# Four kinds of side work beside a transformer: Mamba gets buffers of its own, and the list scheduler reserves accumulator banks for the eldest piece

## The chip, the core and the metric

The kernel runs on one core of a Trainium2 chip. The core has a matrix engine (TensorE, PE in the profile), a vector engine (VectorE, DVE), a scalar engine that evaluates functions (ScalarE, ACT), a programmable engine (GpSimd, POOL) and a queue engine that here issues nearly all DMAs (SyncE, SP). Each engine runs its own instructions in the order in which the program gives them, and waits on semaphores. Matmuls write to PSUM, of which the program has eight banks of 128 x 512 words: seven rotate, one holds small words.

The metric is the device time of one execution in microseconds; lower is better. A measurement is the median of several executions.

## The reference: what is computed

The input `u` is 4 sequences of 1024 positions with 128 channels. Four layers, each as `x = x + layernorm(layer(layernorm(x)))`:

```
# 1 Mamba (selective scan), 16 states
dt = softplus(u W_x[:64] W_dt + b_dt);  B, C = u W_x[64:80], u W_x[80:96]
h[t] = exp(dt[t] * -exp(A_log)) * h[t-1] + dt[t] * u[t] * B[t]
y = sum over states of h * C  +  u * D
# 2 experts: the 2 best of 8 by a router, softmax over the two logits
y = sum over 2 of weight * (gelu(x W_up + b_up) W_down + b_down)     # 128 -> 512 -> 128
# 3 dynamic convolution, 16 heads, 31 taps, causal
w = softmax over taps of (x w_lin);  y[t] = sum over k of w[t, k] * x[t - 30 + k]
# 4 transformer of 6 layers; half of the channels are shifted by one position before each part
for i in range(6):
    x = attention(shift(x)) + x      # 16 heads of 64, windows of 32 and the one before,
                                     # q and k normalised, scaled, rotated
    x = W2 (a * gelu(gate)) + x      # layernorm, 128 -> 2 x 341 -> 128
```

All arrays are float32.

## The kernel before

**Units of work.** A *block* is half a sequence, 512 positions; there are eight, numbered 0 to 7, two a sequence. Mamba, convolution and (in part) the experts work on blocks. A *tile* is 128 positions of one sequence in one transformer layer; there are 4 x 6 x 8 = 192, in order of sequence, layer, position. The transformer can begin with a sequence when both its blocks have gone through Mamba, experts and convolution.

**Three phases.** `sandwich` (L410) makes the generators of the work and merges them. First Mamba on block 0, with the steps of `prepare` (L1141) between its own; then Mamba on block 1, all eight experts on block 0 (`all_experts`, L777) and the rest of `prepare`; then convolution on block 0 and all experts on block 1. Everything else goes along with the transformer, in `Transformer.run` (L1471). `prepare` makes, for each of the six layers, the product of value and output weights (`wvod`) and the scaled rotation tables (`rotd`), and stores them in DRAM, from where each layer loads them later.

**What goes along.** `run` loops over the tiles. For each it turns queries and keys, works out scores, mixes values, and projects the tile after next; after each half sequence of four tiles comes the feed-forward part. Four times a tile it calls `along(i, part)`, which advances the lines of side work. A `Line` (L1564) has a list of jobs with a first and last tile; a job is given out step by step, so that its share of cost follows the share of time. Before the change there are two lines, one of experts and one of everything else (M is Mamba, E experts for two blocks with only the chosen ones, `chosen_experts`, L856; C is convolution):

```
experts = [(E, (2, 3), 18, 30), (E, (4, 5), 56, 78), (E, (6, 7), 84, 118)]
others = [(C, 1, 0, 2.6), (M, 2, 2.6, 11), (M, 3, 11, 18), (M, 4, 18, 30)]
others += [(C, 2, 30, 38), (C, 3, 38, 46), (M, 5, 46, 56), (M, 6, 56, 67)]
others += [(M, 7, 67, 78), (C, 4, 78, 87), (C, 5, 87, 97), (C, 6, 118, 130)]
others += [(C, 7, 130, 144)]
```

**The order on the engines.** None of these calls reaches an engine at once. `Order` (L144) records each as a `Unit` with its engine, an estimated cost, and edges to the units whose data or buffers it needs; matmuls that belong together form one unit. `arrange` (L275) then builds the final order: in each step it looks at the units whose predecessors are all given out, takes on each engine the earliest possible start (and the smallest index among those within `NEAR` of it), and gives out the earliest of all. Three rules bear on the change. A unit may not lie more than `AHEAD` = 500 indices past the oldest one not yet given out. A unit that needs a PSUM bank gets it only if two more stay free, except the oldest such unit. And a bank is fixed only here, when its first unit is given out. On the chip the order on each engine stays as arranged, whatever is late.

**Buffers.** `Rings` (L387) hands out SBUF buffers by tag, `bufs` of them in turn. The tag `near` has three buffers of 128 x 2048 words (`big`, L612). A Mamba block takes all three for its operands, states and products; a convolution tile takes two, one for each half of the 31 taps, and loads its 31 shifted copies of the rows into them by DMA. Both also use the tags `cxn` and `cxT`. Expert weights (514 KB an expert) have three buffers (`ewt`), two loaded ahead.

**Mamba** (`mamba`, L615) is a chain of 16 states: the product of a spread row of B with `dtu` on VectorE, a scan on VectorE (`tensor_tensor_scan`), the product with a spread row of C, and a sum on GpSimd. **Convolution** (`conv`, L1023) does, for each of four tiles, a softmax over taps, four products on GpSimd, two sums on GpSimd, and a sum over taps on VectorE; after the four it normalises and adds the block, stores it, and writes the transformer's input `hs`. **`chosen_experts`** scatters the block's rows into a list by expert (16 indirect DMAs), goes through 23 tiles of the list, fetching each tile's weights by an indirect DMA, and gathers the results. **`layernorm`** (L554) takes statistics on VectorE; it applies them on ScalarE if the source lies in SBUF, and on VectorE, four instructions, if it lies in PSUM.

Almost every instruction carries the line of the recorder that gives it out (L357), so the profile's groups are told apart by their tiles' names.

Of the kernel before, what the change touches and what calls it, by code (L numbers as in the profile page):

```python
# [88 lines left out]
class Bank:  # L89
    def __init__(self, like):  # L90
        self.like, self.ap, self.left, self.writes, self.reads = like, None, 0, [], []


class Unit:
# [4 lines left out]
        "end", "index", "table", "both", "given",  # L99
    )  # L100

    def __init__(self, engine, index):
# [4 lines left out]
        self.table, self.both, self.given = None, False, False  # L107
# [36 lines left out]
class Order:  # L144
# [6 lines left out]
    NEAR = {"tensor": 0.05, "vector": 0.05, "scalar": 0.25, "gpsimd": 0.40, "sync": 1.0}  # L151
    TABLE = {"Exp": "exp", "Gelu": "gelu", "Ln": "ln"}
# [7 lines left out]
    def bank(self):  # L160
        return Late(Bank(self.psum[0]))
# [6 lines left out]
    def take(self, engine, op, args, kw):  # L168
# [7 lines left out]
        if u is None or u.engine != engine:  # L176
            u = Unit(engine, len(self.units))
            self.units.append(u)
            if self.open is not None:
                raise ValueError("another engine in a unit")  # L180
# [20 lines left out]
    forced = None  # L201
# [73 lines left out]
    def arrange(self):  # L275
# [6 lines left out]
        oldest, needy, k_needy = 0, [u for u in units if u.banks], 0  # L282
        free = list(self.free)
        result = []
        while len(result) < len(units):
            while units[oldest].given:
                oldest += 1
            while k_needy < len(needy) and needy[k_needy].given:
                k_needy += 1
            eldest = needy[k_needy] if k_needy < len(needy) else None  # L290
            best = None
            for e, line in ready.items():
                found = []
                for u in line:
# [3 lines left out]
                    if u.banks:  # L298
                        n = len(u.banks)
                        if len(free) < n or (u is not eldest and len(free) < n + 2):  # L300
# [15 lines left out]
            if best is None:  # L316
                raise ValueError("no unit can be given out")
# [12 lines left out]
            for b in u.banks:  # L330
                b.ap = self.psum[free.pop(0)[1]]
# [3 lines left out]
            for b in u.uses:  # L335
                b.left -= 1
                if not b.left:
                    free.append((u.end + 0.08, b.slot))
# [34 lines left out]
class Together:  # L373
# [3 lines left out]
    def __enter__(self):  # L377
        o = self.order
        o.open = Unit("tensor", len(o.units))
        o.units.append(o.open)  # L380
# [29 lines left out]
def sandwich(ctx: ExitStack, tc: tile.TileContext, io: dict, out: bass.AP):  # L410
# [4 lines left out]
    prepare = t.prepare()  # L415
    for _ in c.mamba(0):
        next(prepare, None)
    merge([(c.mamba(1), MAMBA), (c.all_experts(0), ALL), (prepare, 2.0 * DEPTH)])
    merge([(c.conv(0), CONV), (c.all_experts(1), ALL)])
# [24 lines left out]
class Common:  # L444
# [91 lines left out]
    def bank(self, name):  # L536
        return self.nc.bank()
# [16 lines left out]
    def layernorm(self, dst, src, n):  # L554
# [14 lines left out]
        if src.space == PSUM:  # L569
            nc.vector.tensor_copy(mean, mv[:, :, 0])  # L570
            for g in range(n):
                nc.vector.tensor_scalar(
                    dst[:, g, :],
                    src[:, g, :],
                    mean[:, g : g + 1],
                    rs[:, g : g + 1],
                    ALU.subtract,
                    ALU.mult,
                )
        else:  # L580
# [31 lines left out]
    def big(self):  # L612
        return self.sb.tile([P, 4 * BLK], F32, "near", bufs=3)

    def mamba(self, k):  # L615
# [5 lines left out]
        big = [self.big() for _ in range(3)]  # L621
        uT, dt, y, dtu = [big[0][:, i * BLK : (i + 1) * BLK] for i in range(4)]
        ex, w, spare = [big[1][:, i * BLK : (i + 1) * BLK] for i in range(3)]
        parts = big[1][:, 3 * BLK :].bitcast(BF16)[:, :BLK]
        abs_, hs = [[big[2][:, (2 * i + e) * BLK : (2 * i + e + 1) * BLK] for e in range(2)] for i in range(2)]
        hcs = [spare, self.sb.tile([P, BLK], F32, "cxT")]
        dtr = y[:RANK]
        xn = self.norm(x, "m", "cxn")
# [40 lines left out]
        for n in range(STATE):  # L669
            ab = abs_[n % 2]  # L670
            nc.scalar.activation(ab, dt, AF.Exp, scale=self.a_neg[:, n : n + 1])
            h = hs[n % 2]
# [5 lines left out]
                h, ab, db, state if j else 0.0, ALU.mult, ALU.add  # L678
# [1013 lines left out]
```

## Time and profile before

| what | value |
|---|---|
| median of 4 runs | 4307.79 us (4303.37 to 4312.76) |
| the profiled execution | 4303.24 us, of which 4301.1 us from its first to its last instruction (the span) |
| mean granted TensorE clock | 0.945 |
| busy in the span: PE, weight loads, DVE | 3824.6, 2734.8, 3664.0 us |
| busy in the span: ACT, POOL | 2491.6, 2964.2 us |
| DMA | 260.45 MB, mean 61 GB/s |
| scores of tile 0 begin | 355.8 us |

The profile's page gives, by engine, the busy time and its course over 40 equal slices of the span. Other views of the same execution give groups of equal instructions (how many, how long in total and each, and for what the engine stood idle before them), waits by pairs of engines, and busy time by stretches of the span. PE's times are those of matmuls, weight loads have a row of their own and overlap them. A record of an instruction can overlap the next one's, so a group's busy time is less than its count times its mean.

### The profile page before, as it was taken

Reading aid. Unit: us, or ns where it says so; the run is one execution under the profiler, and the core shown is the slowest. Engines: PE = TensorE matmul, PEld = TensorE weight load, DVE = VectorE, ACT = ScalarE, POOL = GpSimd, SP = SyncE. Lnnn points to the kernel's source line nnn. Section 1 sums busy time; section 2 is a strip of 40 time slices with the busy share of each in tenths; the row PEclk is TensorE's granted clock in tenths of the full one; section 3 lists DMA queues with packets and bytes.
Section 4 is the critical chain, followed back from the end, with each engine's and each line's share of the span. In section 5 each row is a group of like instructions: output and inputs, shape, how many; then the busy total and the mean of one; then the engine's idle time right before and its main releaser. Section 6 shows DMA issues by size and latency. Waiting matters only on the chain. (4 is left out here: it accounts for less than half of the span.)

```text
span 4301.1 us, 111840 instructions
## 1 busy us (share of the span) xinstructions
PE 3824.6 (89%) x45298; PEld 2734.8 (64%) x45317; DVE 3664.0 (85%) x9478; ACT 2491.6 (58%) x4572; POOL 2964.2 (69%) x1826
## 2 busy tenths in 40 slices
PE   4856788889889889899998889999999999999997
PEld 2644455667656556577666567776667677777775
DVE  5636899986899899988998978788999998989986
ACT  4533555556555656577655556675556566666654
POOL 4468666675798765767687885666978866666653
PEclk6877899999999999999998999999999999999998
DMA  5522000023212100122122221221121111001010
GB/s 187 179 106 84 21 22 20 22 74 111 80 61 95 44 25 26 44 81 81 42 85 70 77 73 55 67 63 61 64 72 51 54 32 34 30 24 34 26 33 11
DMA packets 131596, 260.45 MB, mean 61 GB/s; under 512 B 15440, under 2 KB 91528, under 8 KB 123144
## 3 DMA queue, kind: packets, MB, share of 16 engines
q1 hardware_dynamic: 118072, 210.68, 14.9%
q0 software_dynamic: 13008, 42.62, 3.3%
q8 instruction: 357, 5.85, 0.6%
q14 instruction: 159, 1.30, 0.1%
HBM read 223.63 MB, written 29.62 MB: 59 GB/s over the span
## 5 line engine op out<-in xcount | busy, mean ns | idle before, releaser
L357 POOL TENSOR_TENSOR r<-r,rb 128x1024 f32<-128x1024 f32 x384 | 909.6, 2376 | 373.5 <-DVE rb L357 307.9
L357 POOL TENSOR_TENSOR r<-r,root 128x1024 f32<-128x1024 f32 x384 | 722.7, 1903 | 195.7 <-DVE root L357 179.3
L357 PE MATMUL bank<-wqk,hs 128*128 128x512 f32 x1536 | 776.0, 630 | 62.6 <-DVE at L357 32.0
L357 PEld LDWEIGHTS bank<-zT,wvo 128*128 128x128 f32 x6144 | 722.7, 194 | 90.4 <-issue 50.5
L357 PE MATMUL bank<-zT,wvo 128*128 128x128 f32 x6144 | 730.1, 277 | 10.5 <-ACT zT L357 8.3
L357 ACT ACTIVATE sq<-bank 128x512 f32<-128x512 f32 x768 | 442.0, 599 | 378.1 <-PE bank L357 191.1
L357 ACT COPY zT<-bank 128x512 f32<-128x512 f32 x768 | 404.7, 594 | 400.1 <-PE bank L357 394.9
L357 DVE TENSOR_TENSOR r<-bank,rot 128x512 f32<-128x512 f32 x768 | 522.9, 681 | 86.5 <-PE bank L357 39.6
L357 POOL TENSOR_TENSOR at<-at,sm 128x1024 f32<-128x1024 f32 x192 | 365.6, 1904 | 310.4 <-DVE sm L357 150.1
L357 DVE TENSOR_TENSOR rb<-bank,rot 128x512 f32<-128x512 f32 x768 | 520.9, 680 | 47.8 <-ACT sq L357 34.5
L357 DVE TENSOR_REDUCE words<-sq 128x8 f32<-128x512 f32 x768 | 526.2, 685 | 12.4 <-ACT sq L357 4.9
L357 PEld LDWEIGHTS bank<-wqk,hs 128*128 128x128 f32 x1536 | 273.5, 197 | 349.9 <-issue 166.7
L357 PE MATMUL bank<-aT,xw 64*128 64x256 f32 x3072 | 443.5, 410 | 21.9 <-DVE near L357 6.2
L357 PE MATMUL bank<-ident,r 128*128 128x128 f32 x3072 | 401.0, 279 | 47.4 <-POOL r L357 23.6
L357 PEld LDWEIGHTS bank<-ident,r 128*128 128x128 f32 x3072 | 353.3, 144 | 131.1 <-issue 63.4
L357 PEld LDWEIGHTS bank<-aT,xw 64*128 64x128 f32 x3072 | 299.2, 194 | 173.6 <-issue 52.5
L357 PEld LDWEIGHTS bank<-kT,qT 64*32 64x32 f32 x24576 | 262.1, 106 | 126.8 <-issue 113.6
L357 ACT COPY qT<-bank 128x512 f32<-128x512 f32 x384 | 226.0, 596 | 176.6 <-PE bank L357 175.2
L357 PE MATMUL bank<-kT,qT 64*32 64x64 f32 x24576 | 300.9, 227 | 21.3 <-issue 21.0
L357 DVE TENSOR_REDUCE mx<-bank 128x8 f32<-128x512 f32 x384 | 255.2, 681 | 68.8 <-PE bank L357 68.5
L357 PE MATMUL bank<-fxn,w 128*128 128x512 f32 (+1 forms) x576 | 275.3, 607 | 9.3 <-ACT fxn L357 5.5
L357 ACT ACTIVATE at<-at 128x1024 f32<-128x1024 f32 x192 | 203.2, 1058 | 119.0 <-DVE at L357 83.9
(180 smaller groups left out, 6781.1 us busy)
## 6 DMA issues: line engine op xcount, KB each, us to landing
near<-rows SPq DMA_DIRECT2D x32, 1024.0 KB
near<-rows SPq DMA_DIRECT2D x32, 960.0 KB
rot<-rotd SPq DMA_DIRECT2D x192, 128.0 KB
wqk<-in_Wqkv SPq DMA_DIRECT2D x48, 512.0 KB
wvo<-wvod SPq DMA_DIRECT2D x24, 1024.0 KB
ewt<-in_w_ex SPq DMA_DIRECT2D x16, 514.0 KB
w<-in_W SPq DMA_DIRECT2D x24, 341.0 KB
rb<-in_rot SPq DMA_DIRECT2D x12, 512.0 KB
```

The lines of the kernel that those rows point to most:

```text
L357: getattr(engine, op)(*map(real, args), **{k: real(v) for k, v in kw.items()})
```

## The change

Six things change together.

1. A Mamba block's operands come from nine buffers of its own (`m0` to `m8`); block 1 borrows the transformer's `r0`, `r1` and `at`, which are not in use yet. It uses `cxn` and `cxT` no more, the scan writes over its own multiplier, and `near` has two buffers. Tags `ewt`, `ey`, `sq` and `xw` lose one of three as well; experts load one ahead in place of two.
2. Four lines go along with the transformer: experts, convolution, Mamba, layer preparation. Mamba on block 2 moves to the phase before, next to convolution on block 0 and the experts on block 1.
3. `prepare` does layer 0 alone; layers 1 to 5 are the fourth line, in halves through the experts' buffers.
4. `layernorm` applies its result on ScalarE for every source.
5. In the first sequence convolution finishes each tile by itself (normalise, add, store, turn), in the others the block as before; the steps are now in `finish`.
6. `arrange`: units that are recorded while lines advance are marked `side`. The oldest unit, from which `AHEAD` counts, is the oldest that is not `side`. The eldest unit that needs banks is kept for each of the two kinds: the elder of the two takes a bank with none to spare, the other with one, all others with two; no more than three banks are held by projections (`qk`); if nothing can be given out, the reserve is waived for that step.

```diff
 class Order:
+    MOST = {"qk": 3}
...
-            while units[oldest].given:
+            while oldest + 1 < len(units) and (units[oldest].given or units[oldest].side):
                 oldest += 1
-            while k_needy < len(needy) and needy[k_needy].given:
-                k_needy += 1
-            eldest = needy[k_needy] if k_needy < len(needy) else None
+            for line in needy:
+                while line and line[-1].given:
+                    line.pop()
+            eldest = [line[-1] for line in needy if line]
+            first = min(eldest, key=lambda u: u.index, default=None)
...
-                        if len(free) < n or (u is not eldest and len(free) < n + 2):
+                        if len(free) < n + (0 if u is first or stuck else 1 if u in eldest else 2):
+                            continue
+                        name = u.banks[0].name
+                        if held.get(name, 0) >= self.MOST.get(name, 9):
                             continue
...
-    prepare = t.prepare()
-    for _ in c.mamba(0):
-        next(prepare, None)
-    merge([(c.mamba(1), MAMBA), (c.all_experts(0), ALL), (prepare, 2.0 * DEPTH)])
-    merge([(c.conv(0), CONV), (c.all_experts(1), ALL)])
+    merge([(c.mamba(0), MAMBA), (t.prepare(), 4.0)])
+    merge([(c.mamba(1), MAMBA), (c.all_experts(0), ALL)])
+    merge([(c.conv(0), CONV), (c.all_experts(1), ALL), (c.mamba(2), MAMBA)])
...
         if src.space == PSUM:
-            nc.vector.tensor_copy(mean, mv[:, :, 0])
-            for g in range(n):
-                nc.vector.tensor_scalar(
...
-        else:
+            pass
+        if True:
             nc.vector.scalar_tensor_tensor(mean, mv[:, :, 0], -1.0, rs, ALU.mult, ALU.mult)
...
     def big(self):
-        return self.sb.tile([P, 4 * BLK], F32, "near", bufs=3)
+        return self.sb.tile([P, 4 * BLK], F32, "near", bufs=2)
...
-        big = [self.big() for _ in range(3)]
...
+        if k == 1:
+            pairs = [self.sb.tile([P, 2, BLK], F32, f"r{i % 2}", bufs=2) for i in range(4)]
+            pieces = [pair[:, e, :] for pair in pairs for e in range(2)]
+            parts = self.sb.tile([P, 2, BLK], F32, "at", bufs=2)[:, 0, :]
+        else:
+            pieces = [self.sb.tile([P, BLK], F32, f"m{i}") for i in range(8)]
+            parts = self.sb.tile([P, BLK // 2], F32, "m8")
...
             nc.vector.tensor_tensor_scan(
-                h, ab, db, state if j else 0.0, ALU.mult, ALU.add
+                h, h, db, state if j else 0.0, ALU.mult, ALU.add
             )
...
-            w = self.sb.tile([P, 2 * UP + NUC], F32, "ewt", bufs=3)
+            w = self.sb.tile([P, 2 * UP + NUC], F32, "ewt", bufs=2)
...
-        ahead = [fetch(0), fetch(1)]
+        ahead = [fetch(0)]
...
-            if i + 2 < nt:
-                ahead.append(fetch(i + 2))
+            if i + 1 < nt:
+                ahead.append(fetch(i + 1))
...
+        size = 1 if b == 0 else 4
...
+            if g % size == size - 1:
+                self.finish(k, x, y, slice(g + 1 - size, g + 1))
...
+    def prepare_layer(self, l):
+        for j in range(2):
+            both = self.sb.tile([P, 8, D], F32, "exn")
+            wv, wo = both[:, :4], both[:, 4:]
+            dma(out=wv, in_=io["WvT"][l][:, 4 * j : 4 * j + 4])
...
+            for e in range(2):
+                wvo = self.sb.tile([P, BLK], F32, "eT")
+                nc.scalar.copy(wvo, pair[e])
+                dma(
+                    out=self.wvod[l][:, e, 4 * j : 4 * j + 4, :].rearrange("p a d -> p (a d)"),
+                    in_=wvo,
+                )
...
-        experts = [(E, (2, 3), 18, 30), (E, (4, 5), 56, 78), (E, (6, 7), 84, 118)]
+        experts = [(E, (2, 3), 8, 26), (E, (4, 5), 52, 70), (E, (6, 7), 98, 118)]
+        mambas = [(M, 3, 0, 8), (M, 4, 10, 32), (M, 5, 32, 52), (M, 6, 52, 74), (M, 7, 74, 98)]
+        convs = [(C, 1, 0, 2.6), (C, 2, 26, 35), (C, 3, 35, 44), (C, 4, 70, 80), (C, 5, 80, 90), (C, 6, 118, 127), (C, 7, 127, 138)]
+        layers = [((self.prepare_layer, 4.0), l, 1.6 * l - 1.6, 1.6 * l) for l in range(1, DEPTH)]
+        lines = [Line(experts, [1.45, 1.0, 0.05, 1.5])]
+        lines += [Line(jobs, [1.1, 1.0, 0.8, 1.1]) for jobs in (convs, mambas, layers)]
...
         def along(i, part):
+            c.nc.side = True
             for line in lines:
                 line.advance(i, part)
+            c.nc.side = False
```

## The prediction

> **What bounds the kernel now.** I read the page first. (PE is TensorE, DVE VectorE, ACT ScalarE, POOL GpSimd, SP the queue that issues most DMAs; the digits are busy tenths of 40 slices.)
>
> ```profile
> span 4301.1 us, 111840 instructions
> ...
> PE 3824.6 (89%) x45298; PEld 2734.8 (64%) x45317; DVE 3664.0 (85%) x9478; ACT 2491.6 (58%) x4572; POOL 2964.2 (69%) x1826
> ...
> PE   4856788889889889899998889999999999999997
> DVE  5636899986899899988998978788999998989986
> ...
> POOL 4468666675798765767687885666978866666653
> PEclk6877899999999999999998999999999999999998
> ```
>
> No engine is full over the span, but PE and DVE are each near 9 tenths from slice 6 on; the first five slices, about 540 us, hold PE at 4 to 8 and DVE at 3 to 6, with a throttled clock. So there are two stages, each to be costed by itself. I cut the span where the transformer's tiles begin: the mask matmul of tile 0's scores starts at 355.8 us, that of tile 8 at 562.9, and the later cuts (tiles 18, 30, 46, 56, 78, 97, 118, 144, 184) are where the program's due times change what goes along. The view by stretches, with busy us and (instructions) of PE, weight load, DVE, ACT, POOL, then clock and DMA:
>
> ```profile
> 0.00:356.00 356.00, 217.92 (x1174) 162.06 (x1176) 200.83 (x522) 158.10 (x311) 184.37 (x156) 0.77 0.45 153
> 356.00:563.00 207.00, 149.35 (x1716) 101.05 (x1716) 158.07 (x344) 96.74 (x173) 156.28 (x91) 0.84 0.12 38
> 563.00:792.00 229.00, 200.80 (x2271) 131.19 (x2273) 220.06 (x557) 128.24 (x219) 148.32 (x93) 0.96 0.08 25
> 792.00:1116.00 324.00, 291.07 (x3146) 213.98 (x3150) 251.60 (x654) 191.81 (x414) 209.12 (x149) 0.93 0.24 72
> 1116.00:1449.00 333.00, 293.68 (x3539) 199.21 (x3537) 312.38 (x824) 180.63 (x318) 288.57 (x162) 0.95 0.22 77
> 1449.00:1661.00 212.00, 190.33 (x2295) 129.76 (x2296) 195.31 (x503) 127.55 (x225) 131.84 (x84) 0.97 0.09 25
> 1661.00:2157.00 496.00, 463.60 (x5401) 336.68 (x5404) 449.90 (x1141) 331.32 (x630) 349.12 (x232) 0.97 0.20 59
> 2157.00:2572.00 415.00, 356.48 (x4329) 253.07 (x4328) 361.09 (x985) 226.96 (x413) 340.67 (x201) 0.93 0.23 77
> 2572.00:2981.00 409.00, 400.25 (x5012) 298.82 (x5011) 336.70 (x890) 270.79 (x515) 261.66 (x163) 0.99 0.20 58
> 2981.00:3462.00 481.00, 453.13 (x5769) 317.18 (x5768) 449.96 (x1176) 283.71 (x498) 387.92 (x217) 0.99 0.18 62
> 3462.00:4130.00 668.00, 662.40 (x8839) 486.05 (x8837) 606.85 (x1550) 408.66 (x712) 428.77 (x241) 1.00 0.10 30
> ```
>
> The last line is the transformer alone: 40 tiles in 668 us, 16.7 us a tile, PE at 99%, DVE 607/40 = 15.2, POOL 429/40 = 10.7. That is the price of a tile. In 563 to 792 (two Mamba blocks along) DVE is at 96%, in 2572 to 2981 (experts) PE at 98%. In 792 to 1116 and 2157 to 2572 neither is over 90%: time is lost. One loss has a name in the view of waits for 2440 to 2500, where TensorE stood for a token list that GpSimd had scattered late:
>
> ```profile
> PE bank L357 <- DMA exs<-listed: 25.2, 1, 25.2
> ```
>
> The prices of what goes along are in the groups (count, then busy us, mean ns, idle before):
>
> ```profile
> L357 DVE TENSOR_TENSOR bank<-bank,near 128x512 f32<-128x512 f32 x128 | 87.2, 692 | 18.5 <-POOL near L357 9.6 <-PE bank L357 8.1
> ...
> L357 DVE TENSOR_TENSOR_SCAN near<-near,carry,bank 128x512 f32<-128x512 f32 x64 | 81.0, 1270 | 1.4 <-ACT near L357 0.7
> ...
> L357 DVE TENSOR_SCALAR fxn<-bank,mean,rs 128x128 f32<-128x128 f32 x192 | 65.9, 402 | 0.3
> ...
> L357 POOL TENSOR_TENSOR near<-near,ew 128x1024 f32<-128x1024 f32 x96 | 203.8, 2137 | 4.4 <-DMA near<-rows 3.6
> ...
> L357 PE MATMUL bank<-exsT,ewt 128*128 128x128 f32 x552 | 77.2, 284 | 8.7 <-ACT exsT L357 3.2 <-DVE near L357 2.3 <-DVE words L357 1.7
> ```
>
> Busy us over the count is the price, since records overlap. A Mamba block, an eighth of its groups: DVE 54 (products and scans 332.5/8 = 41.6, the rest and two norms 12.4), POOL 29.6, PE 12. A conv block: POOL 56.2, DVE 31.6, PE 5. A group of chosen experts (23 tiles): PE 50, POOL 56.5, DVE 34.
>
> **The change part by part.**
> *Norms of PSUM sources* (62 of them): four DVE instructions of 343 ns busy share and a copy go, one of 158 ns comes: 1.37 us less DVE a norm, four ACT instructions of about 0.41 us more. One norm falls on four tiles: DVE 14.85 a tile in place of 15.2, ACT 0.4 more. ACT is 61% busy in the last stretch, which covers that. There PE is full, so a tile stays at 16.7 and this part is worth nothing in the tail; it counts only where DVE binds.
> [...] I go by the row: slack of 1.5 us a tile on DVE and none between matmuls.
>
> *Mamba's own buffers and four lines.* Mamba no longer shares the gather buffers with conv, so block 2 moves into the opening and block 3 into tiles 0 to 8; the others stretch over 20 to 24 tiles in place of 10 to 12, beside conv and experts. I add, per stretch of the due times in the code, the tile price and each job's share, and take the largest engine. Before (tiles 8, 18, 30, 46, 56, 78, 97, 118, 144): 225, 270, 306, 206, 476, 365, 382, 458, sum 2689; measured 562.9 to 3462.2 is 2899, 1.078 times as much. Then 40 tiles at 16.7 give the measured 668. After (tiles 8, 26, 44, 52, 70, 90, 98, 118, 138): 359 (PE), 376 (DVE), 140, 360 (PE), 405 (DVE), 138, 384 (PE), 360 (DVE), sum 2522, then 46 tiles at 16.7, 768. One of them in full, tiles 26 to 44: DVE 18 x 14.85 = 267, two conv blocks 63, 6/22 of Mamba block 4 and 12/20 of block 5 (52.6 each now) 46, together 376. The 25.2 us above came from scattering while conv's products sat on POOL; in the changed program's order every group scatters (tiles 10 to 14, 54 to 57, 100 to 104) with no conv beside it. So I take (2899 - 25)/2689 = 1.069: 2522 x 1.069 + 768 = 3464 against 3567 to the same tile 184, **-103**. Factors of 1.03 (the best mixed stretch, 212/206) and 1.11 bound it: -201 and 0.
>
> *The opening pays for it.* Each DVE instruction of the changed order, priced by its group, gives 251 us before tile 0's scores (197 before) and 213 from tile 0 to 8 (160): 464 in place of 356. The 108 more are block 3, the rest of block 2, and 16 one-tile norms in place of four four-tile ones (each 13 small instructions of about 0.15 us). The chain up to the first experts' end stays: block 0 to 84 us, experts to 192, with 107 us of DVE work done by then. 357 remain. At 95% (DVE's share in the Mamba stretch) they end at 568; at 77% (its share in 356 to 563) at 656. I take 87.5%, 600, nearer the first because Mamba's scans are ready whenever conv(1) makes the main line wait: **+37** (+5 to +93). What is late next is conv(1): with two gather buffers each of its four tiles goes load, four products, two sums, reduction in turn, some 6 + 13 + 4 = 23 us and more beside POOL's other work, but now each tile is finished by itself, and tile 4 waits for one of them in place of four.
>
> *Layer preparation.* Five of six layers leave the first 200 us for tiles 0 to 8: 3.5 us PE, 2.4 ACT, 4.7 POOL a layer, and 14 DMAs in place of 8. With 6 more stores of conv, SP issues 42 more at about 0.4 us, 17 us on a queue that mostly waits. Behind a store that waits for ACT's copy stand rotation rows and conv's gathers; in the opening SP's waits were of 5 to 23 us. I cost it at nothing, since rows are issued a tile ahead; uncovered, five layers' four stores at 2 us are 40 us, kept for the range.
>
> *Fewer buffers* (gather 3 to 2, expert weights 3 to 2, results, squares and windows 3 to 2). Now the weights of tile i+1 are fetched only when tile i-1 is done. In the trace's packets the 69 fetches end 3.7 to 7.4 us after issue, 4.0 in the median; with the products (1.8 us) the least period is about 6 us, 138 us of the 360 that a group has. The changed order sets four or five tiles between two scores only at tiles 16, 21, 60 and 61: 17 tiles x 6 - 4 x 20 = 22 us of stall at most; it is inside the factor, since tile 25 before had 12. [...]
>
> *Banks.* The eldest piece of the other line now needs one spare bank, others two, and a projection at most three. The trace shows no wait by banks as such; I take 0, and keep +-20 us (about a tenth of the 185 us that weight loads stood for ACT's zT and DVE's at, 107.0 + 78.2 in the view of waits, which could have been for a bank).
>
> Sum: 4301 - 103 + 37 = 4235 of span. The profiled execution took 4303.2 with 4301.1 of span, and the runs' median is 4307.8, 4.6 more: **4242**.
>
> **Rivals.**
> A. *Expert weights bind* (slower). Place: the three groups, 69 tiles. PE's order is fixed, so a late fetch holds up the main line too. For: a fetch waits on PE's last product and on GpSimd's queue, where instructions of 2.4 us stand before it; in the burst at 968 to 984 us weights came only 0.5 to 1.5 us early with two ahead. Against: from 1748 on they came 5 to 70 us early. Price: 2 us a tile, 138 us, 4380. It decides at 66/69 = 1 us a tile.
> B. *The opening eats the gain* (no change). POOL, with 384 us priced up to tile 8, holds conv(1); DVE stays at 77%, tile 8 comes at 656, and the factor stays at 1.078 (-80): 4301 + 93 - 80 = 4314, some 4320.
> C. *All of it pays*: factor 1.04 (-177) and tile 8 at 568: 4129, some 4136. For: 46 to 56 ran at 1.03. Against: the two conv stretches before lost most after the experts' (333/306 and 415/365), and tiles 26 to 44 now hold conv and Mamba, POOL at 18.4 us a tile beside DVE's 20.9.
> D. *The lines do nothing*, since side work still runs when its data come: then only the norms count, 0.35 x 136 tiles where DVE binds at most half, 24 us: 4284.
>
> **Numbers.** Runs of before span 4303 to 4313, so 0.2% (9 us) is what can be told from no change. Chances: forecast 0.48, D 0.10, C 0.10, B 0.14, A and other stalls 0.18. Faster: 0.48 + 0.10 + 0.10 = 0.68; B is split, half of it within 9 us; A is slower: same 0.07, slower 0.25. The range leaves out most of A and half of C: 4160 to 4350; the forecast's own is 4190 to 4290.
>
> **What would show it.** Right: tile 8 near 600 us with DVE over 85% from 192 on; the mixed tiles at 20 us, none over 35; 46 last tiles at 16.7 with PE at 99%; DVE's total some 45 us lower. Wrong: PE waiting for weights or lists in tiles 14 to 24, 59 to 69, 105 to 117; SP waiting for ACT in the opening while rows or gathers are late; last tiles above 16.9, which would blame two square buffers or the three banks.

## The result: no gain, and what the profile after shows

The changed kernel takes 4308.8 us in the median, the one before 4304.2 us in the runs beside it: a ratio of 1.0009, with an interval of 1.0004 to 1.0013. 4242 us was forecast. The profiled execution of the changed kernel took 4310.2 us, 4308.1 of it span. Its page, with the rows that were shown of before:

```profile
span 4308.1 us, 112030 instructions
...
PE 3828.3 (89%) x45302; PEld 2723.2 (63%) x45317; DVE 3611.1 (84%) x9374; ACT 2582.1 (60%) x4835; POOL 2964.4 (69%) x1832
...
PE   3875699998989898999888999999898999999997
DVE  4787788689989898779989898678899898888985
...
POOL 3388657568887657668978567567878566666663
PEclk6886899999989999999989999999999999999998
```

DVE lost 53 us of work and ACT gained 90, the way the edit to the norms moves it; PE's work is the same. To see where the time stayed, both spans are cut at the same tiles (the mask matmul of tiles 0, 8, 144 and 184):

| us | before | after | forecast |
|---|---|---|---|
| up to tile 0 | 355.8 | 329.4 | - |
| tiles 0 to 8 (tile 8 starts at) | 207.1 (562.9) | 271.2 (600.6) | 600 |
| tiles 8 to 144 | 2899.3 | 2865.4 | 2796 |
| tiles 144 to 184 | 668.2 | 672.2 | 668 |
| the rest | 170.7 | 170.0 | 171 |

(2796 is 2522 x 1.069 and six tiles at 16.7.) Tile 8 started when it was forecast to. The mixed part, tiles 8 to 144, gained 34 us where 103 were forecast. By the new due times, in the view by stretches (busy us and instructions of PE, weight load, DVE, ACT, POOL, then clock and DMA):

```profile
329.00:601.00 272.00, 184.08 (x1910) 119.02 (x1910) 202.22 (x548) 121.21 (x218) 191.75 (x115) 0.80 0.34 113
601.00:1001.00 400.00, 373.27 (x4469) 277.22 (x4472) 328.50 (x844) 268.33 (x550) 275.19 (x181) 0.99 0.24 72
1001.00:1392.00 391.00, 347.79 (x4039) 233.74 (x4041) 359.30 (x907) 227.74 (x406) 330.38 (x193) 0.95 0.20 68
1392.00:1558.00 166.00, 145.84 (x1826) 101.31 (x1824) 151.37 (x444) 100.30 (x184) 97.70 (x59) 0.96 0.10 32
1558.00:1961.00 403.00, 375.68 (x4446) 274.15 (x4446) 327.20 (x809) 269.06 (x541) 272.15 (x182) 0.96 0.22 66
1961.00:2404.00 443.00, 386.35 (x4497) 258.19 (x4496) 402.81 (x1016) 251.94 (x449) 363.73 (x213) 0.93 0.18 61
2404.00:2544.00 140.00, 134.78 (x1784) 97.84 (x1782) 129.22 (x378) 89.59 (x164) 86.82 (x50) 1.00 0.11 32
2544.00:2956.00 412.00, 394.28 (x4873) 295.91 (x4872) 319.41 (x831) 267.67 (x538) 259.68 (x169) 0.98 0.22 67
2956.00:3354.00 398.00, 356.04 (x4423) 246.95 (x4422) 356.57 (x923) 228.00 (x411) 332.59 (x188) 0.96 0.20 69
3354.00:3466.00 112.00, 108.76 (x1374) 77.57 (x1373) 95.38 (x244) 71.53 (x129) 64.15 (x38) 1.00 0.10 28
3466.00:4138.00 672.00, 658.76 (x8820) 484.84 (x8819) 595.92 (x1503) 420.04 (x747) 426.34 (x241) 1.00 0.10 30
```

Lines 2 to 9 are tiles 8 to 138, priced at 359, 376, 140, 360, 405, 138, 384 and 360 us. They took 1.11, 1.04, 1.19, 1.12, 1.09, 1.01, 1.07 and 1.11 times as much, 1.092 together; 1.069 was taken. Part of the difference is work that was priced too low. The busiest engine of each of these eight lines was busy for 2548 us together, 26 more than the 2522 priced; the three expert stretches, where that engine is PE (lines 2, 5 and 8), held 1143 us against 1103. In the eight lines of before from 563 us on, the same sum is 2697, for 2689 priced. The time was 1.081 times the busy sum after and 1.075 times before, so no less time was lost beside the busiest engine, although the list wait of 25 us is gone.

Tiles 8 to 144 in one cut, first before, then after:

```profile
563.00:3462.00 2899.00, 2649.34 (x31749) 1879.89 (x31763) 2576.99 (x6722) 1741.03 (x3226) 2117.22 (x1296) 0.96 0.19 60
```

```profile
601.00:3466.00 2865.00, 2622.79 (x31717) 1862.89 (x31725) 2469.76 (x6392) 1774.16 (x3366) 2082.39 (x1266) 0.97 0.20 62
```

DVE has 107 us less to do, part of it moved into the opening, and the part is 34 us shorter. PE was busy 91.4% of it before and 91.5% after. Beside what a lower clock adds to its matmuls (0.96 was granted on average; in tile 36 of the changed kernel a pair of conv's products took 1.10 us at 1.00 and 2.02 at 0.50), only 250 us of idle PE time were there to be won, and the forecast asked for 40% as much.

No wait took over. The forecast's list wait is gone (PE before gathered rows, 25.8 us, now 2.2), and PE never stood for expert weights. What PE waits for is spread over many short waits. The first rows of its view of waits for the whole span, before and after:

```profile
PE bank L357 <- ACT cxn L357: 85.2, 5, 55.6
PE bank L357 <- DVE near L357: 62.7, 42, 12.8
PE bank L357 <- DVE at L357: 45.6, 39, 4.2
```

```profile
PE bank L374 <- DVE m L374: 71.6, 55, 11.4
PE bank L374 <- DVE at L374: 45.8, 35, 5.9
PE bank L374 <- DVE rb L374: 37.6, 40, 5.2
PE bank L374 <- ACT m L374: 34.0, 6, 15.8
PE bank L374 <- ACT qT L374: 32.7, 31, 16.2
PE bank L374 <- ACT eT L374: 30.2, 14, 4.5
```

(The numbers are the us in total, the times, and the longest one.) The first row of before lies for 71 of its 85 us ahead of the transformer. Apart from it and the list wait, no single wait in these rows is longer than 16.2 us. The attention's own buffers (at, rb) cost about as much as before; Mamba's buffers (near before, which conv shares, m after) more; and eT, in which the layer preparation stages its products, is new as a wait of this size (1.5 us before). Some tiles became long. Tile 36 took 43.9 us, with a conv group and Mamba along; the view by stretches of it, in the same columns:

```profile
1204.00:1216.00 12.00, 7.07 (x148) 3.40 (x147) 11.27 (x22) 7.09 (x10) 11.77 (x9) 0.99 0.01 2
1216.00:1228.00 12.00, 5.99 (x8) 1.61 (x8) 10.53 (x14) 1.44 (x2) 12.00 (x9) 0.50 0.00 1
1228.00:1240.00 12.00, 9.65 (x26) 5.48 (x27) 8.23 (x9) 4.73 (x8) 10.61 (x7) 0.52 0.28 89
1240.00:1248.00 8.00, 6.99 (x61) 6.51 (x61) 5.76 (x18) 3.39 (x8) 3.38 (x3) 1.00 0.36 138
```

In the second line PE has 8 matmuls in 12 us and its granted clock is 0.50, after 0.99 in the first. POOL is busy throughout, some 7.6 us of it with conv's instructions, and DVE for 10.5 us, nearly all with Mamba's and conv's instructions.

### The profile page after: what moved, and what is told of

It is laid out like the page before. It is cut to its first block, busy times and chain, and to the rows that moved or that the text cites. A ratio compares the mean times of both kernels' runs of the same rounds, so it can differ in the third digit from the quotient of the medians.

```text
span 4308.1 us, 112030 instructions
## 1 busy us (share of the span) xinstructions
PE 3828.3 (89%) x45302; PEld 2723.2 (63%) x45317; DVE 3611.1 (84%) x9374; ACT 2582.1 (60%) x4835; POOL 2964.4 (69%) x1832
## 3 DMA queue, kind: packets, MB, share of 16 engines
q1 hardware_dynamic: 123352, 211.47, 15.2%
## 5 line engine op out<-in xcount | busy, mean ns | idle before, releaser
L374 PE MATMUL bank<-wqk,hs 128*128 128x512 f32 x1536 | 779.7, 627 | 65.8 <-DVE at L374 21.2
```

The lines of the kernel that those rows point to most:

```text
L374: getattr(engine, op)(*map(real, args), **{k: real(v) for k, v in kw.items()})
```

## The experiments

The theories at the start were: side pieces that collide on POOL and VectorE, the new bank rule, and the fewer buffers. Each kernel's ratio is to the kernel before, run beside it. "Mixed" is tiles 8 to 144 in its trace (before 2899, after 2865 us), "opening" tiles 0 to 8 (207 and 271). These stage times come from one trace each. e1 to e4 and e9 to e11 ran on a chip on which the kernel before takes 4283 to 4286 us and not 4304, so their stages look shorter beside the traces of before, after and e7; spread evenly, that is 12 to 14 us of the mixed part. This is an estimate, and "set right" below means with it. Ratios are free of it.

**The bank rule, and the buffers, each alone.** e1 adds the rule (the whole of point 6 of the change, of which these are the main lines) to the kernel before:

```diff
-                        if len(free) < n or (u is not eldest and len(free) < n + 2):
+                        if len(free) < n + (0 if u is first or stuck else 1 if u in eldest else 2):
+                        if held.get(name, 0) >= self.MOST.get(name, 9):
```

> The kernel before with the new bank rule alone: banks kept for the eldest piece of the tiles and of the side work, at most three qk banks held, and the 500-piece window measured from the oldest piece of the tiles. Due times, buffers, opening and norms are those of before. Theory 'collision' (the stretches at tiles 8 to 138 run at 1.092 of their priced work because whole side pieces now go side by side on POOL and VectorE): within 10 us of before, 4295 to 4315. Theory 'bank rule' (the rule lets side work take banks and engines ahead of the tiles, and that costs the 58 us by which the factor was missed): 4325 to 4360. The forecast had 0 +- 20 us for this term.

0.9987 (0.9977 to 0.9997), 6 us; mixed 2852, opening 231. e2 takes the rule out of the changed kernel:

> The changed kernel with the old bank rule (one eldest piece, two banks in reserve for it, the 500-piece window measured from the oldest of all pieces, no limit on qk banks). Theory 'collision': 4295 to 4320, long tiles at 36, 78, 81 and 124 stay (35 us or more). Theory 'bank rule': 4240 to 4285, and those tiles fall under 30 us. A third way, that the rule is needed for four lines to go along (side pieces that wait for a bank hold the window): 4330 to 4400.

1.0187 (1.0170 to 1.0204), 77 us over the changed kernel; mixed 2914, opening 282. So the rule shortens the mixed part in both kernels, by 47 and 49 us as measured, by some 35 and 61 set right; in the kernel before it costs the opening 24, most of what it gains. My theory that it holds the tiles up falls; the changed kernel needs it. Which of its parts pays, the banks kept back, the limit on qk or the window of 500 that no longer counts side work, is not shown.

e3 cuts the buffers of the kernel before:

```diff
-                sq = self.sb.tile(half, F32, "sq", bufs=3)
+                sq = self.sb.tile(half, F32, "sq", bufs=2)
-        xw = self.sb.tile([P, 4, P], F32, "xw", bufs=3)
+        xw = self.sb.tile([P, 4, P], F32, "xw", bufs=2)
-            w = self.sb.tile([P, 2 * UP + NUC], F32, "ewt", bufs=3)
+            w = self.sb.tile([P, 2 * UP + NUC], F32, "ewt", bufs=2)
-        ahead = [fetch(0), fetch(1)]
+        ahead = [fetch(0)]
...
```

> The kernel before with fewer buffers alone: sq and xw two instead of three, expert weights two and fetched one ahead, ey two. Theory 'small buffers' (ScalarE waits twice as long before sq, 215.5 us against 103.9, and the last tiles take 16.8 us where 16.7 was forecast): 4320 to 4350, the last 40 tiles at 16.8 or more. Theory 'collision': 4298 to 4315, last 40 tiles at 16.7, the longer wait of ScalarE is slack. The forecast bounded the expert weights at 22 us.

1.0173 (1.0153 to 1.0194), 73 us; mixed 2969, 70 more than before (82 set right). 53 of these lie in tiles 18 to 26, where tile 21 took 80 us: PE stood 21.2 us before the rows gathered for the first expert tile. e5 cuts sq and xw alone:

> The kernel before with two sq and two xw buffers instead of three, and nothing else; expert weights stay three and fetched two ahead. The kernel with all buffers cut lost 73 us, 53 of them in tiles 18 to 26, where TensorE stood 21 us before the rows gathered for the first expert tile; its last 40 tiles took 16.80 us each against 16.68. Theory 'sq holds ScalarE' (wait of ScalarE on VectorE's row sums goes from 72 to 174 us in the mixed part): last 40 tiles again at 16.8, 15 to 35 us over before in all, no stop at tiles 18 to 26. Theory 'the cut of sq and xw also set off the stop': 60 to 75 us over before. Theory 'all of it is weights': within 8 us of before, last tiles at 16.68.

1.0077 (1.0060 to 1.0094), 33 us; mixed 2925. The same stop is there (tile 21 took 75 us), in the waits of 800 to 960 us, tiles 18 to 22, of PE and of GpSimd:

```profile
PE bank L357 <- DMA exs<-listed: 20.8, 1, 20.8
POOL ewt L357 <- ACT exsT L357: 18.9, 1, 18.9
```

Tiles 18 to 26 took 28 us more and the rest of the mixed part 2 less, so beside the stop these buffers cost nothing there. Their last 40 tiles took 16.8 us each, but so did those of e11, which has three of each (16.8); those of all kernels lie between 16.6 and 16.9. The tail says nothing on the buffers, and "sq holds ScalarE" falls. Of e3's 73 us, some 40 came with the cut of the experts' weights and results (ewt, ey): 1.0173 against 1.0077.

e6 was to give the changed kernel a third sq, at the price of one ehg buffer (three in place of four). The experts of blocks 0 and 1 have four in use at a time, so one inner layer is written over before it is read, which changes the computation.

> The changed kernel with three sq buffers, paid for with one of the four buffers that hold the experts' inner layer (ehg, three instead of four), nothing else. Theory 'sq holds ScalarE': 10 to 30 us faster than the changed kernel (1.0009 of before becomes 0.994 to 0.9985), wait of ScalarE for the row sums back from 215.5 to about 110 us, last 40 tiles at 16.7 instead of 16.80. Theory 'collision of side pieces': within 8 us of the changed kernel, since the wait is slack.

1.0189 (1.0172 to 1.0206); with the fourth ehg buffer gone it says nothing on sq. e9 found room without that (conv's rows in the experts' buffers), on top of e7 below:

> The kernel of e7 (changed kernel, all layers prepared before the transformer) with three sq and three xw buffers again; the room comes from conv, whose normalised and turned rows use the experts' buffers (exn, eT), which stand empty while conv works. Theory 'sq holds ScalarE': ScalarE's wait for the row sums falls from 216 to about 110 us, the last 40 tiles from 16.8 to 16.65 to 16.7, and the whole is 10 to 30 us faster than e7 (0.9964 of before becomes 0.989 to 0.994). In the kernel before, the same cut cost 33 us, of which 28 were the one stop at tiles 18 to 26. Theory 'only that stop cost anything': within 8 us of e7.

1.0079 (1.0062 to 1.0096), 49 us slower than e7's ratio. ScalarE's wait for the row sums fell from 216.4 to 66.0 us (about 110 was expected), and nothing came of it; mixed rose from 2857 to 2891 (by 48 set right), with stops at tiles 42 (60 us) and 103 (50 us; PE stood 22.5 us of it before gathered rows). So the wait alone is not what costs. Whether the shared conv buffers caused the stops is open.

**The lines alone.** e4 gives the changed kernel the due times of before:

```diff
-        experts = [(E, (2, 3), 8, 26), (E, (4, 5), 52, 70), (E, (6, 7), 98, 118)]
-        mambas = [(M, 3, 0, 8), (M, 4, 10, 32), (M, 5, 32, 52), (M, 6, 52, 74), (M, 7, 74, 98)]
+        experts = [(E, (2, 3), 18, 30), (E, (4, 5), 56, 78), (E, (6, 7), 84, 118)]
+        others = [(C, 1, 0, 2.6), (M, 3, 2.6, 18), (M, 4, 18, 30)]
...
-        lines += [Line(jobs, [1.1, 1.0, 0.8, 1.1]) for jobs in (convs, mambas, layers)]
+        lines += [Line(jobs, [1.1, 1.0, 0.8, 1.1]) for jobs in (others, layers)]
```

> The changed kernel (Mamba's own buffers, opening with Mamba 2, norms, rule, fewer buffers) with the due times of before: Mamba and conv one after the other in one line, experts at tiles 18 to 30, 56 to 78 and 84 to 118, the layers in a line of their own. If the lines themselves are worth what the priced sums say (67 us to tile 184, of which the chip showed 30): 4335 to 4375. If conv and Mamba side by side cost as much in stalls as the balance gives (theory 'collision'): 4295 to 4320. The opening is shorter by the work of Mamba 3, which now has until tile 18 instead of 8: tile 8 near 570 us by either.

1.0090 (1.0073 to 1.0107), 35 us over the changed kernel; mixed 2917 (64 more than the changed kernel, set right), opening 243. The range of the priced sums was reached at its lower end, but see e16.

**The norms.** e8 puts them back on VectorE in the changed kernel, e11 adds them to e1.

> The changed kernel with the normalisation out of PSUM on VectorE again (248 pieces of 128x128 back from ScalarE). The forecast put about 45 us of VectorE work on this, all of it in stretches where VectorE is the most loaded, and nothing in the tail. If that work is on the path: 15 to 40 us slower than the changed kernel (1.0045 to 1.010 of before). If ScalarE's waits eat it: within 8 us of the changed kernel; if ScalarE in order is what stalls the stretches, 10 to 25 us faster.

> The kernel before with the new bank rule and the normalisation out of PSUM on ScalarE, and nothing else: three buffers of everything, two lines, the old opening. The rule alone gave 0.9987 of before. The norms were worth 47 us in the changed kernel (1.0117 without, 1.0009 with them). If that holds where Mamba's lines are the old ones, 0.985 to 0.992 (4240 to 4270 on a chip where before takes 4304). If the norms only pay where VectorE and TensorE are equally loaded, 0.994 to 0.9985.

e8: 1.0117 (1.0094 to 1.0140), mixed 2938, opening 243. e11: 0.9994 (0.9985 to 1.0004), mixed 2852, as in e1 without the norms, though DVE's work there fell from 2573 to 2519 us. The mixed part of e1 and of e11, on the same chip:

```profile
588.00:3440.00 2852.00, 2628.32 (x31764) 1859.48 (x31772) 2573.16 (x6715) 1735.57 (x3224) 2114.82 (x1293) 0.97 0.19 61
```

```profile
590.00:3442.00 2852.00, 2624.45 (x31758) 1864.15 (x31756) 2518.95 (x6510) 1793.27 (x3402) 2110.44 (x1290) 0.96 0.19 61
```

The same edit is worth 47 us in one kernel and nothing in the other: this edit has no price of its own here.

**Is it POOL?** e10 leaves out conv's sum of its two halves on POOL, so that DVE sums the first half alone:

```diff
-            for k0, k1 in ((0, 8), (8, CK - half)):
-                nc.gpsimd.tensor_tensor(
-                    out=flat[0][:, k0:k1],
-                    in0=flat[0][:, k0:k1],
-                    in1=flat[1][:, k0:k1],
-                    op=ALU.add,
-                )
```

> The changed kernel without conv's sum of its two halves on POOL (two pieces a group, 128x1024 and 128x896, 4.46 us; 17.8 us a block, 143 us in all, of which 107 at tiles 26 to 138 and 18 in the opening): VectorE then sums the first half alone. That addition is what is left out. In conv's stretches (tiles 26 to 44, 70 to 90, 118 to 138) POOL has 0.82 to 0.84 of the time as work and VectorE 0.90 to 0.93. Theory 'the most loaded engine sets a stretch': at most 10 us less in those stretches together, 5 to 15 us in the opening. Theory 'balance': a second engine nearly as loaded as the first raises the factor (1.02 to 1.07 where it has 0.77 to 0.87 of the first, 1.10 to 1.30 where it has 0.95 and more), so that each stretch loses 10 to 25 us, 30 to 75 us in the three, and the long tiles 36, 78, 81 and 124 fall under 35 us.

0.9959 (0.9945 to 0.9973), 21 us; tiles 26 to 44, 70 to 90 and 118 to 138 took 390, 426 and 404 us (391, 442, 398 with it), so 107 us of POOL work are worth 11 there, some 5 set right. That is the theory of the most loaded engine; "balance" falls. In the opening 18 us less on POOL brought tile 8 from 600.6 to 565.6 (by some 32 us set right).

**The layers.** e7 prepares them before the transformer, on the gather buffers:

```diff
-            both = self.sb.tile([P, 8, D], F32, "exn")
+            piece = c.big()
+            both = piece[:, : 2 * BLK].rearrange("p (a d) -> p a d", d=D)
...
-                wvo = self.sb.tile([P, BLK], F32, "eT")
+                wvo = piece[:, (2 + e) * BLK : (3 + e) * BLK]
...
-        yield from self.prepare_layer(0)
+        for l in range(DEPTH):
+            yield from self.prepare_layer(l)
```

> The changed kernel with all six layers prepared before the transformer, beside Mamba 0 and 1 and the experts of block 0 as before, on the two gather buffers (near), which no other work uses there; the fourth line is gone. Theory 'layers in the opening': tiles 0 to 8 took 271 us, in which TensorE did 20 products of weights at up to half clock and ScalarE waited 35.9 us for its one staging buffer to be stored; without them 236 to 250 us, tile 0 at 329 to 345, the whole 10 to 30 us faster than the changed kernel. Theory 'Mamba 3 in the opening': tiles 0 to 8 stay at 262 to 271 us and the whole within 8 us or slower, since the layers were in gaps.

0.9964 (0.9952 to 0.9977), faster than both kernels. Tile 18 starts at 806.2 us (825.1 in the changed kernel); from there on both take 2529 us to tile 138. e18 also sums conv's halves of blocks 0 and 1 on VectorE:

> The kernel of e7, in which conv of blocks 0 and 1 sums its two halves on VectorE (two sums over 16 and 15 rows and one addition of 128x128) and not first on POOL; the result is the same sum. In e10 the opening fell by 35 us (tile 8 from 600.6 to 565.6) when POOL's additions were left out, 17.8 us of them in the opening. VectorE gets about 4 x 4 us more there for 4 x 4.46 us less on POOL. If POOL sets the opening: tile 8 at 565 to 580 instead of 590, the whole 10 to 25 us under e7 (0.990 to 0.994 of before), give or take the scatter of 10 to 40 us that the nudges showed. If VectorE sets it as much: within 8 us of e7 but for that scatter.

0.9973 (0.9961 to 0.9984): no gain over e7. Tile 8 came at 587 against 590; VectorE got what POOL gave up.

**How much is chance?** e12 to e14 nudge the scheduler and change no work (e12, e13: one constant by 0.01 or 0.02 us; e14: Mamba's line asked ahead of conv's); e15 repeats e14's swap on e7, e16 and e17 repeat e13's nudge on e4 and e7.

> The kernel before with one constant of the list scheduler moved by a hair: among VectorE pieces that can start within 0.06 us of each other the eldest is taken, where it was 0.05. No work, buffer, due time or rule differs, only the order that the scheduler comes out with. Theory 'scatter' (each plan stops somewhere for 30 to 60 us by chance, and any edit deals these stops anew): the time moves by 15 to 60 us either way. Theory 'each edit has its own price' (norms 47 us, sq and xw 33 us): within 6 us of before.

> The changed kernel with the same kind of nudge on POOL: 0.42 us instead of 0.40. Theory 'scatter': 15 to 60 us away from the changed kernel (1.0009 of before becomes 0.987 to 1.015), with other long tiles than 36, 78, 81 and 124. Theory 'each edit has its own price': within 6 us.

> The changed kernel with Mamba's line ahead of conv's where both are due in the same quarter of a tile; due times, work and rule stay. Theory 'scatter': 15 to 60 us away from the changed kernel, in either direction, by other stops. Theory 'each edit has its own price': within 6 us; if conv's pieces ahead of Mamba's chain are what stops tiles 36, 78 and 81, 15 to 40 us faster with those tiles under 32 us.

> The kernel of e7 (layers prepared before the transformer) with the same swap of the two lines. If the swap has a price of its own, it differs from e7 (0.9964 of before) by what e14 differs from the changed kernel, within 6 us. Theory 'scatter': the two differences have nothing to do with each other.

> The kernel of e4 (changed kernel with the two lines and due times of before) with the nudge of e13 (0.42 us on POOL). With e4 this gives the worth of the four lines on two plans: e4 was 35 us over the changed kernel. If the four lines are worth what the priced sums say (67 us to tile 184), this is 30 to 90 us over e13 (1.0069 of before becomes 1.014 to 1.028). If e4's 35 us were scatter, it is within 25 us of e13 either way, 1.001 to 1.013.

> The kernel of e7 with the nudge of e13. The layers ahead of the transformer were worth 19 us on the changed kernel's plan (e7) and 43 us on the swapped one (e15 against e14). If that gain is the edit's own (ScalarE no longer waits for its staging buffer in the opening), this is 10 to 45 us under e13: 0.9965 to 1.0045 of before. If both were scatter, it is as likely over e13 as under it.

| | plain | nudged | swapped |
|---|---|---|---|
| before | 1 | e12 1.0025 (1.0012 to 1.0037) | |
| changed | 1.0009 | e13 1.0069 (1.0052 to 1.0086) | e14 1.0104 (1.0087 to 1.0120) |
| two lines | e4 1.0090 | e16 1.0067 (1.0051 to 1.0084) | |
| layers early | e7 0.9964 | e17 0.9988 (0.9978 to 0.9998) | e15 1.0001 (0.9992 to 1.0011) |

A nudge that changes no work moves the time by 10 to 41 us. In the changed kernel the scatter is not spread over the span: its tiles 18 to 138 and those of e7, e13 and e17 took 2529 to 2531 us, of the two swapped ones 2537 and 2541. Most of it sits before tile 18. e13 lost its time in tile 14 (65 us), where expert tiles came in a bunch and PE did stand for weights, in two waits:

```profile
PE bank L374 <- DMA ewt<-in_w_ex,ewidx: 10.0, 2, 5.0
```

Read by rows of the table: preparing the layers early is worth 19, 35 and 44 us on three plans, each time before tile 18, so it is very likely a gain of its own. The four lines against two are worth 35 and -1 us: not shown to be worth anything.

## Why the prediction was wrong

**What bounds the kernel**: right, and read too weakly. The working had PE at 91% and DVE at 89% of tiles 8 to 144 in its own lines, and priced each stretch by its largest engine. In that part a gain has to come out of PE's idle time, and the working never looked at how much there was: 250 us. Taking 107 us of work off DVE left PE's share where it was.

**The step that failed is the factor** on the priced sum, 1.069 for 8 to 138. It measured 1.092, 58 us. Some 28 of them are the work that was priced too low (26 us, times the factor). The rest is time lost beside the busiest engine: the working took off 25 us for the list wait, that wait went away, and as much was lost elsewhere. The 46 last tiles at 17.0 in place of 16.7 add 16 us, 12 of them in tiles 138 to 144, which took 112 us with PE busy for 109, so they are not the lone tiles that the last 40 are. Which edit kept the factor up is not shown. Two terms that were put inside it or at nothing were wrong where they could be measured alone:

- *Fewer buffers, at most 22 us.* Cut in the kernel before, they cost 73 us, 53 of them in tiles 18 to 26, around one stop at the first expert tiles. That is beyond the scatter of the nudges, 41 us at most; the 33 us of sq and xw alone (e5) are not. The expected cause (PE waits for weights fetched one ahead) was absent in the changed kernel and small elsewhere, 7 us in e3 and 10 in tile 14 of e13: bounding the cost by that one cause was the mistake. How much of it the changed kernel pays could not be isolated, since there is no room to give the buffers back without another change. In e3 the cut showed in single long stops (21.2 us of PE before the gathered rows in one wait, for 7.0 us before the weights in three) more than in a repeated gap, and cost three times the 22 us.
- *Banks, 0 +- 20.* The rule gains 6 us of the whole in the kernel before and 77 in the changed one. In tiles 18 to 138, where nudges and swaps move 1 to 14 us, it is worth 47 and 43 us as measured, some 37 and 54 set right. No such gain was in the sum, so the other terms missed by more than the total shows. With the rule alone the mixed part of the kernel before gets 35 us shorter, set right; the whole change makes it 34 shorter. So all of that gain can be had by the rule, and what the other edits do there adds up to nothing.

**The lines** (the rest of the -103): 35 us on one plan, -1 on another. **Norms**: nothing in the tail, as said; tiles there went from 15.2 to 14.9 us of DVE and stayed at 16.7 to 16.8, with PE busy for 659 of the 672 us of tiles 144 to 184, so the row that the working went by was right. Taken out of the changed kernel they cost 47 us in all (73 in the mixed part, the opening got 28 shorter); in the kernel before with the rule they are worth nothing.

**The opening, +37**: tile 8 at 600.6, but through two errors that cancel. From 192 us on DVE had 313 us of work, not 357, and was 77% busy, not 87.5:

```profile
192.00:601.00 409.00, 290.82 (x2412) 194.55 (x2416) 312.99 (x865) 203.16 (x383) 299.56 (x191) 0.82 0.34 114
```

**Layer preparation at nothing** was a further miss, with 40 us kept as its bound: 19 to 44 us. The wait that was named did come, SP behind ACT's copies, but ACT stood longer behind the store of its one staging buffer, and PE behind ACT. In the views of waits, 329 to 601 us:

```profile
ACT eT L374 <- DMA wvod<-eT: 35.9, 9, 4.6
PE bank L374 <- ACT eT L374: 23.8, 11, 4.2
```

```profile
SPq L374 <- ACT eT L374: 22.5, 8, 5.1
```

**Signs named in advance**: tile 8 near 600 held; DVE over 85% before it did not; "mixed tiles none over 35 us" did not (36, 81, 78, 56, 124, 69 and 45 took 35 to 44); PE at 98% in the last tiles and DVE's total, 53 us lower, nearly did. Last tiles above 16.9 were to blame the square buffers or the banks: the 46 took 17.0 each, but so did the same tiles before. **Rivals**: A did not come (0 us of waits for weights); B ends nearest, 4320, and had DVE's 77% right, but tile 8 not at 656 and the factor not at 1.078; D's 4284 is 25 us off, C far.

Open: why the factor is 1.09 in tiles 26 to 138 (2353 us for 2163 priced) on every plan of these lines. Taking away the rule, the norms or POOL's sums, moving the layers or giving sq and xw back did not bring tiles 18 to 138 down by more than 15 us of 2529; the gather buffers, the weights fetched one ahead and Mamba's two states that are written in place could not be undone for want of room.

## What to carry to other kernels

Before summing the largest engine of each stretch, look at the idle time of the engine that the main line runs on: that, and what a lower clock adds to its work, is all there is to win while that work stays the same (here 250 us of 2899, beside matmuls such as the pair that took 2.02 us at a granted 0.50 and 1.10 at 1.00). Here VectorE had 107 us less to do and the part became 34 us shorter, which one rule of the scheduler gave by itself. A buffer that is given up is cheaply priced by cutting it in the old kernel, on its own. Where a list scheduler makes the order, nudge it without changing any work first: differences below its scatter (10 to 41 us here, most of it in one or two stops) cannot be told from the plan's. By that measure e2 and e3 stand clear in the whole time; the others count only where several plans, or the quieter tiles 18 to 138, agree.

## What the runs showed of the hardware

PE's granted clock fell from 1.00 to 0.50 while PE was working, only thinly. In tile 36 PE had 3.7 us of matmuls in the 8 us from 1208 to 1216 (46%), with no gap over 1.8 us, and the granted clock went to 0.50 at about 1215.7 for the 24 us that followed. The gap of 2.59 us below came after the fall. The same pair of products for conv took 1.10 us before and 2.02 us after it:

```profile
1209.19 1.10 PE L374 MATMUL bank<-wl,cxT 128*128 128x496 f32 x2 [1.77 <-DVE at L374]
1210.13 0.60 PE L374 MATMUL bank<-ident,at 128*128 128x128 f32 x4
1211.41 0.66 PE L374 MATMUL bank<-ident,at 128*128 128x128 f32 x4 [0.68 <-ACT aT L374]
1212.36 0.75 PE L374 MATMUL bank<-m,sel 128*128 128x512 bf16 x2 [0.30 <-DVE m L374]
1214.07 0.38 PE L374 MATMUL bank<-m,sel 128*128 128x512 bf16 x1 [0.95 <-DVE m L374]
1215.37 0.38 PE L374 MATMUL bank<-m,sel 128*128 128x512 bf16 x1 [0.92 <-DVE rb L374]
1218.33 2.02 PE L374 MATMUL bank<-wl,cxT 128*128 128x496 f32 x2 [2.59 <-DVE m L374]
```

So here PE first stood behind DVE and then ran slower matmuls. That the waits brought the clock down is my estimate, from their order in time alone: no run shows what set it.
